# Gated cross attention and mixture of experts: weights and token kept behind each quarter of a row, slot loads on one queue, the last gates by TensorE

## The chip, the cores and the metric

The kernel runs on one core of a Trainium2 chip. The metric is the device time of one execution in microseconds, the median of three runs. A core has a matrix engine (TensorE, PE), a vector engine (VectorE, DVE), a scalar engine (ScalarE, ACT), a general engine (GpSimd, POOL) and a sync engine (SyncE, SP). Each has its own instruction stream and works through it in order; they wait for each other with semaphores. Transfers are issued by SP, ACT and POOL and carried by 16 DMA engines.

## The reference

`x` is 4 x 2048 x 512 in float32, 8192 tokens in all; the context is 4 x 77 x 512. A gated cross attention with 16 heads of 64 is followed by a gated mixture of 8 true and 2 null experts, of which each token takes the best two.

```python
x = x + tanh(g_xattn[0]) * xattn(layernorm(x), ctx)      # q, k, v, softmax over 77 keys, w_out, b_out
h = layernorm(x)
logits = h @ gate_w.T + gate_b                           # 10 columns: 8 experts, 2 null
weights, selected = top_k(softmax(logits), 2)
true = weights * (selected < 8)
combine = one_hot(selected) * true / max(sum(true), ...)  # per token and expert
x = x + tanh(g_ffn[0]) * sum_e combine[:, e] * (h @ expert_w[e] + expert_b[e])
```

## The kernel before, in words

**First phase.** Keys are folded into the query weights and values into the output weights, so that one tile of 128 tokens needs only two groups of matmuls: scores (line 281, four chunks of 512 by 1232 columns) and the attention output (line 360, ten chunks into one PSUM bank, `attend`). There are 64 tiles; `step(i)` works on several at a time: scores of tile i+1, attend of tile i-1, gates of tile i-2. The order of all instructions is written out by hand (`manual_schedule`), so each engine's order is the order of the calls. The softmaxed scores are transposed in 32 x 32 squares by VectorE and put in place by 16 small transfers from SP (`attn_move`, line 353).

**Gates and buckets.** After the residual (line 373) and its store, tile i's normalised row is written by ScalarE into one of nine row buffers of 528 columns (`norm_apply`, line 255): 512 of data, then two weights and the token number. `gate_logits` (line 382) makes ten products with reductions on VectorE, one per gate; `choose` finds the best two, `ratio` and `weigh` make the weights, `place` (line 453) counts with two small matmuls, `dispatch` computes row numbers and scatters the rows of two tiles into two buckets in HBM, `hb[0]` for first choices and `hb[1]` for second (line 475, GpSimd, indirect). Each bucket has room per expert, so rows of one expert stand together.

**Second phase.** Rows are worked in slots of 128 rows of one expert: 118 of them, 59 of the first choices and then 59 of the second. Each pass ends with eight "part" slots whose rows are gathered through an index. `early_table`, `first_table` and `second_table` compute on VectorE where each slot starts and which expert it has. For a slot: `slot_load` brings its rows from `hb`, in an arrangement that makes VectorE's 32 x 32 transpose (`slot_tr`, line 943) a full one; `slot_acc` gathers the tokens' present output (line 925, GpSimd); `slot_pe` makes four matmuls of 512 columns (line 981); `slot_out` adds bias, scales and adds (lines 989, 990, VectorE); `slot_put` scatters the result (line 997, GpSimd). Part slots are transposed by TensorE with two ScalarE copies (lines 952 to 958).

A full slot's load is five transfers: one for the columns behind the data (line 902) and four for the quarters of 128 columns (line 905). After slot 8 two of the quarters go by ScalarE's queue. There are eleven slot buffers: seven row buffers and four pieces of the softmax buffers; loads are issued five slots ahead, transposes two.

**Hand-over.** The first slots need only tiles up to SNAP (57), so slots 0 to 3 are mixed with attend 62 and 63. In this stretch VectorE makes the gate products of tiles 61 and 62, and `tail(q)` does tile 63's, two products per slot, its dispatch and the first table at q = 8, the second table at q = 12 and the part table at q = 14.

Of the kernel before, what the change touches and what calls it, by code (L numbers as in the profile page):

```python
# [8 lines left out]
F32 = mybir.dt.float32  # L9
# [15 lines left out]
def kernel(  # L25
# [112 lines left out]
    for n in range(2):  # L138
        a = const.tile([P, NKC * P], F32, name=f"attn{n}")
        nc.gpsimd.memset(a[:, COLS:], 1.0)  # L140
        attns.append(a)
    rows = []
    for n in range(NRB):
        r = const.tile([P, ROW], F32, name=f"row{n}")
        nc.gpsimd.memset(r[:, D:], 0.0)
        rows.append(r)

    nc.gpsimd.memset(rows[0][:, :D], 0.0)
    nc.gpsimd.memset(rows[0][:, D + 2 : D + 3].bitcast(I32), BIG)
# [103 lines left out]
    def norm_apply(key, dst, src):  # L253
        rs, nb = norms.pop(key)
        nc.scalar.activation(dst, src, AF.Identity, bias=nb, scale=rs)

# [120 lines left out]
    def gate_logits(i, e0, e1):  # L377
        if e0 == 0:
            pgs[i] = stile("pg", i, NG)
        for e in range(e0, e1):  # L380
            prod = work.tile([P, D], F32, tag="prod", name=f"prod_{i}_{e}", bufs=1)
            nc.vector.tensor_tensor_reduce(  # L382
                prod,
                hrs[i][:, :D],
                gwb[:, e, :],
# [5 lines left out]
            )  # L391

# [5 lines left out]
    def choose(i):  # L398
# [25 lines left out]
        nc.gpsimd.tensor_copy(hrs[i][:, D + 2 : D + 3].bitcast(I32), tokid[:, i : i + 1])  # L424
# [9 lines left out]
    def weigh(m):  # L434
# [9 lines left out]
        for b in range(2):  # L444
            nc.vector.tensor_scalar(
                hrs[2 * m + b][:, D : D + 2], w2[:, b], rd[:, b : b + 1], gf, ALU.mult, ALU.mult
            )

    def place(m):

        pps[m] = pp = mm_tile(f"pp{m}")
# [9 lines left out]
    def dispatch(m):  # L461
# [10 lines left out]
        for i in (2 * m, 2 * m + 1):  # L472
            hr = hrs.pop(i)
            for k in range(2):
                ins = nc.gpsimd.indirect_dma_start(  # L475
                    out=hb[k],
                    out_offset=bass.IndirectOffsetOnAxis(ap=dst[:, i % 2, k : k + 1], axis=0),
                    in_=hr[:, :].bitcast(I32),
                    in_offset=None,
                    bounds_check=NROWS - 1,  # L480
                    oob_is_err=False,
                )
                tc.declare_no_dep(ins.ins, group="scatter", reason="rows of one bucket differ")
                tc.add_to_no_dep_group("scatter", ins.ins)
                if i > SNAP:
                    tc.declare_no_dep(ins.ins, group="block", reason="blocks full by tile SNAP")
                    tc.add_to_no_dep_group(f"late{i}", ins.ins)
# [185 lines left out]
    def step(i):  # L673
# [14 lines left out]
        if i == NT - 2:  # L688
            slot_tr(0)
            slot_tr(1)  # L690
# [26 lines left out]
        if is_tile(i - 1):  # L717
            norm_shift(f"h{i - 1}")
            hrs[i - 1] = rows[(i - 1) % NRB]
            norm_apply(f"h{i - 1}", hrs[i - 1][:, :D], x1s.pop(i - 1))  # L720
# [53 lines left out]
    scr = m_flat[:, 6 * D :]  # L774
    assert NT * (2 * NE + 1) <= NC * COLS - 6 * D

    def count_rows(cs):
        pc = mm_tile("pc")
# [92 lines left out]
    ring += rows[NRB - 3 : NRB - 1]  # L871
    px_pool = []
    hss, metas, toks, accs, hsTs, exps, pes, turn = {}, {}, {}, {}, {}, {}, {}, [0, 0]

    def slot_load(n):
# [3 lines left out]
        metas[n] = hs[:, D:]  # L879
# [9 lines left out]
        else:  # L889
            both = n > N1 // 2  # L890
            queues = (nc.sync, nc.scalar) if both else (nc.sync,)
            r = nc.values_load(
                starts[t][0:1, s : s + 1],
                engines=[ENG.SP, ENG.Activation] if both else [ENG.SP],
# [7 lines left out]
            loads = [queues[0].dma_start(hs[:, D:].bitcast(I32), block[:, D:])]  # L902
            for g in range(4):
                loads.append(
                    queues[g // 2 * (len(queues) - 1)].dma_start(  # L905
                        hs[g * 32 : (g + 1) * 32, :D]
                        .rearrange("p (j d) -> p j d", j=4)
                        .bitcast(I32),
                        block[:, g * P : (g + 1) * P].rearrange("(j a) d -> a j d", a=32),
                    )  # L910
                )
            if t == 0:
# [6 lines left out]

    def slot_acc(n):  # L920
        k = order[n][0]
        tok = metas[n][:, 2:3].bitcast(I32)
# [272 lines left out]
```

## Time and profile before

| | us |
|---|---|
| runs | 1693.61, 1693.76, 1691.02 (median 1693.61) |
| profiled execution | 1677.89 |
| its span | 1676.2 |
| granted TensorE clock, mean | 0.993 |
| one slot on TensorE (distance between starts) | 3.43 |
| one attend on TensorE | 8.59 |

The profile is of one execution. A line of instructions in time has start, duration, engine, line, operation, output<-input, shape and count, and in brackets the idle time before it with what ended it. A line of a group has the busy total, the mean duration in ns and the idle time before it. TensorE's busy time holds overlapping durations (a group of eight records shows 3.60 where the next starts 3.43 later), so distances between starts are used.

### The profile page before, as it was taken

To read this page: it belongs to the slowest core of one execution; us is meant where nothing else is said; L and a number is where in the kernel's file an instruction comes from. 1 tells how busy PE (TensorE), PEld (TensorE's weight loads), DVE (VectorE), ACT (ScalarE), POOL (GpSimd) and SP (SyncE) were. 2 spreads that over 40 slices of the span, in tenths; PEclk is the share of its full clock that TensorE was granted. 3 is DMA by queue.
4 is the path that set the end of the run, shared out by engine and by line. 5 is a ranking of instruction groups with operands and counts; after the bars stand their busy time and mean duration, and the time that the engine had idled before them with its cause. 6 is when DMAs were issued, how large, how long until landed. Compare 5 with 4: busy or idle time off the path is not lost.

```text
span 1676.2 us, 23173 instructions
## 1 busy us (share of the span) xinstructions
PE 1635.7 (98%) x4530; PEld 809.5 (48%) x4530; DVE 1293.8 (77%) x3324; ACT 884.2 (53%) x3188; POOL 466.9 (28%) x617
## 2 busy tenths in 40 slices
PE   8899999999999999999999999999988999999997
PEld 6544455454544545455454554545433444444443
DVE  1554999899898998989899898998988755466653
ACT  2464777777777777767777677776620000100001
POOL 4031111112111211112111121111226656575565
PEclk9999999999999999999999999999998999999999
DMA  7468443346533445644333566655447986688862
GB/s 236 177 198 228 105 98 87 85 104 162 153 89 85 107 94 144 154 93 107 88 94 88 154 169 145 162 139 160 112 112 229 266 242 187 173 255 235 233 189 78
DMA packets 484934, 252.07 MB, mean 150 GB/s; under 512 B 369509, under 2 KB 425829, under 8 KB 484529
## 3 DMA queue, kind: packets, MB, share of 16 engines
q1 hardware_dynamic: 423473, 134.77, 34.4%
q0 software_dynamic: 34528, 103.55, 18.8%
q10 hardware_dynamic: 26784, 12.20, 3.0%
q14 instruction: 109, 0.89, 0.2%
q8 instruction: 40, 0.66, 0.2%
HBM read 119.41 MB, written 100.52 MB: 131 GB/s over the span
## 4 chain that ended last, share of the span: by engine, by line
PE 85%; DVE 5%; DMA 3%; SPq 3%; issue 2%; ACT 1%; POOL 1%; POOLq 0%; DVEq 0%; ACTq 0%
PE po L360 29%; PE sc L281 29%; PE px L981 11%; PE pe L981 10%; PE pv L622 2%; SPq L353 2%; DVE prod L382 2%; PE pkv L519 2%; PE xtr L261 2%; DMA vw_all<-row 1%; DMA gwb<-in_L_ffn_gate_w_dram 1%; DMA x<-in_x_dram 0%; DMA row<-hb 0%; SPq L905 0%; PE pm L597 0%
## 5 line engine op out<-in xcount | busy, mean ns | idle before, releaser
L360 PE MATMUL po<-vw,aT 128*128 128x512 f32 (+1 forms) x1280 | 561.8, 594 | 2.6 <-issue 2.4
L281 PE MATMUL sc<-m_sb,xnT 128*128 128x385 f32 (+1 forms) x1536 | 552.9, 510 | 0.0
L382 DVE CUSTOM_DVE_ANT_0 prod<-row,gwb,gbias 128x512 f32<-128x512 f32 x640 | 478.3, 747 | 25.2 <-DMA gwb<-in_L_ffn_gate_w_dram 7.3
L360 PEld LDWEIGHTS po<-vw,aT 128*128 128x128 f32 (+1 forms) x1280 | 243.8, 191 | 305.3 <-issue 301.9
L281 PEld LDWEIGHTS sc<-m_sb,xnT 128*128 128x128 f32 x1536 | 283.9, 190 | 212.5 <-issue 86.1
L475 POOL DMA_INDIRECT hb<-row,dst x128 | 128.1, 1001 | 752.1 <-DVE nbh_h L250 673.0
L314 ACT ACTIVATE attn<-sc,nmx 128x77 f32<-128x77 f32 x1024 | 316.0, 346 | 35.0 <-DVE nmx L309 31.3
L314 ACT ACTIVATION_READ_ACCUMULATOR attn<-sc,nmx 128x1 f32 x1024 | 232.8, 227 | 0.0
L981 PE MATMUL px<-big,m_sb 128*128 (+1 forms) x472 | 215.1, 599 | 10.7 <-DVE m_sb L943 10.4
L981 PE MATMUL pe<-big,m_sb 128*128 (+1 forms) x472 | 212.5, 593 | 1.0 <-DVE m_sb L943 1.0
L981 PEld LDWEIGHTS px<-big,m_sb 128*128 128x128 f32 x472 | 89.7, 192 | 121.7 <-issue 109.2
L981 PEld LDWEIGHTS pe<-big,m_sb 128*128 128x128 f32 x472 | 88.8, 190 | 110.1 <-issue 106.4
L303 DVE TENSOR_REDUCE mx<-sc 128x5 f32<-128x385 f32 (+1 forms) x192 | 106.2, 580 | 20.2 <-PE sc L281 18.1
L233 ACT ACTIVATE sdh_h<-mvh_h,eps_t 128x1 f32<-128x1 f32 x64 | 18.9, 295 | 187.7 <-DVE rsa_a L245 178.5
L989 DVE TENSOR_TENSOR yb<-pe,blks 128x512 f32<-128x512 f32 x59 | 40.6, 688 | 76.9 <-PE pe L981 76.9
L952 ACT COPY m_sb<-row 128x512 f32<-128x512 f32 x11 | 6.8, 620 | 176.4 <-DVE acc L990 174.5
L264 ACT ACTIVATE xnT<-xtr,bet,gam 128x128 f32<-128x128 f32 x256 | 95.4, 452 | 7.4 <-PE xtr L261 7.4
L989 DVE TENSOR_TENSOR yb<-px,blks 128x512 f32<-128x512 f32 x59 | 40.6, 688 | 76.0 <-PE px L981 74.6
L327 DVE TENSOR_TENSOR attn<-attn,ri 128x1232 f32<-128x1232 f32 x64 | 92.3, 1443 | 5.1 <-DMA aT<-attn 0.8
L997 POOL DMA_INDIRECT out_dram<-acc,row x75 | 76.2, 1016 | 65.1 <-DVE acc L990 52.2
L336 DVE STREAM_TRANSPOSE attn<-attn 128x1248 f32<-128x1248 f32 x64 | 94.2, 1471 | 0.0
L373 DVE SCALAR_TENSOR_TENSOR x<-po,gx,x 128x512 f32<-128x512 f32 x64 | 48.0, 750 | 58.0 <-PE pp L453 34.5
(163 smaller groups left out, 1540.1 us busy)
## 6 DMA issues: line engine op xcount, KB each, us to landing
aT<-attn SPq DMA_DIRECT2D x768, 40.0 KB
x<-in_x_dram SPq DMA_DIRECT2D x64, 256.0 KB
out_dram<-x SPq DMA_DIRECT2D x64, 256.0 KB
aT<-attn SPq DMA_DIRECT2D x256, 36.0 KB
row<-hb SPq DMA_DIRECT2D x138, 64.0 KB
big<-in_L_ffn_expert_w_dram SPq DMA_DIRECT2D x32, 256.0 KB
row<-hb ACTq DMA_DIRECT2D x118, 64.0 KB
vw<-vw_all SPq DMA_DIRECT2D x9, 768.0 KB
```

What stands on the lines that cost most here:

```text
L264: nc.scalar.activation(xnT[:, c, :], ptr[:, c, :], AF.Identity, bias=bet[:, c : c + 1], scale=gam[:, c : c + 1],)
L281: nc.tensor.matmul(t[:, : n1 - n0], xnTs[i][:, c, :], m_sb[:, c, n0:n1], start=(c == 0), stop=(c == NC - 1),)
L303: nc.vector.tensor_reduce(mx[:, g0:g1], scs[i, g][:, : (g1 - g0) * SK].rearrange("p (h k) -> p h k", k=SK), AX.X, ALU.max,)
L314: nc.scalar.activation(a[:, h * SK : (h + 1) * SK], t[:, k : k + SK], AF.Exp, bias=nm[:, h : h + 1], scale=SCALE, accum_out=sm[:, h : h + 1],)
L327: nc.vector.tensor_tensor(a, a, ri.unsqueeze(2).to_broadcast([P, H, SK]), ALU.mult)
L336: nc.vector.transpose(a[:, :n], a[:, :n])
L360: nc.tensor.matmul(po, aT[:m, k, :], vw[:m, k, :], start=(k == 0), stop=(k == NKC - 1),)
L382: nc.vector.tensor_tensor_reduce(prod, hrs[i][:, :D], gwb[:, e, :], 1.0, gbias[:, e : e + 1], ALU.mult, ALU.add, pgs[i][:, e : e + 1],)
L475: ins = nc.gpsimd.indirect_dma_start(out=hb[k], out_offset=bass.IndirectOffsetOnAxis(ap=dst[:, i % 2, k : k + 1], axis=0), in_=hr[:, :].bi ...
L981: nc.tensor.matmul(pe, hsT[:, c, :], w[:, c, :], start=(c == 0), stop=(c == NC - 1))
L989: nc.vector.tensor_tensor(tt, pe, b, ALU.add)
L997: ins = nc.gpsimd.indirect_dma_start(out=of, out_offset=bass.IndirectOffsetOnAxis(ap=tok, axis=0), in_=acc, in_offset=None, bounds_check=T ...
```

## The change

- A row is now four quarters of 132 columns: 128 of data, two weights, the token, one unused. The weights and the token are written behind each quarter (`weigh`, `choose`), the token as a float. Everything that reads or writes the data of a row uses a view of four pieces.
- A full slot's load is four transfers of 132-column quarters, all by SP. A new `slot_meta` copies, on ScalarE, the pieces behind the quarters to the place of the first one and turns the token to an integer.
- There are twenty slot buffers (nine pieces of the value buffer are added); loads are issued nine slots ahead, transposes of full slots four.
- The gates of tiles 61, 62 and 63 are made by TensorE: the gate weights are transposed once before step 4, and for each tile `gate_transpose` and `gate_product` are called in the hand-over.
- The order of the hand-over is new: slot 1 after attend 62, loads of slots 3 to 6 after the moves of tile 63, tile 63's dispatch before slot 6 with its four scatters spread over q = 1 to 4, the tables at q = 3, 6 and 9. Small counts use the transpose banks, and slots use the two kinds of PSUM bank in groups of three.

```diff
+    QC = D // 4
+    QR = ROW // 4
+    def quarters(r):
+        return r.rearrange("p (i d) -> p i d", d=QR)
...
+    def norm_row(i):
+        hrs[i] = rows[i % NRB]
+        norm_apply(
+            f"h{i}",
+            quarters(hrs[i])[:, :, :QC],
+            x1s.pop(i).rearrange("p (i d) -> p i d", i=4),
+        )
...
             nc.vector.tensor_tensor_reduce(
-                prod,
-                hrs[i][:, :D],
-                gwb[:, e, :],
+                prod.rearrange("p (i d) -> p i d", i=4),
+                quarters(hrs[i])[:, :, :QC],
+                gwb[:, e, :].rearrange("p (i d) -> p i d", i=4),
...
+    def setup_gate():
+        rows10 = rows[NRB - 1][:, :D]
+        ptr = tr_tile("gwtr")
+        for c in range(NC):
+            nc.tensor.transpose(ptr[:, c, :NG], rows10[:NG, c * P : (c + 1) * P], ident[:NG, :NG])
+        nc.vector.tensor_copy(gwT, ptr[:, :, :NG])
+
+    def gate_transpose(i):
+        ptr = tr_tile(f"gtr{i}")
+        for c in range(NC):
+            nc.tensor.transpose(ptr[:, c, :], quarters(hrs[i])[:, c, :QC], ident)
+        nc.scalar.copy(hgT, ptr)
+
+    def gate_product(i):
+        pl = tr_tile(f"gl{i}")[:, 0, :NG]
+        for c in range(NC):
+            nc.tensor.matmul(pl, hgT[:, c, :], gwT[:, c, :], start=(c == 0), stop=(c == NC - 1))
+        pgs[i] = stile("pg", i, NG)
+        nc.vector.tensor_tensor(pgs[i], pl, gbias, ALU.add)
...
+    ring += [vw_flat[:, v * ROW : (v + 1) * ROW] for v in range(NKC * D // ROW)]
...
-            both = n > N1 // 2
-            queues = (nc.sync, nc.scalar) if both else (nc.sync,)
...
-            loads = [queues[0].dma_start(hs[:, D:].bitcast(I32), block[:, D:])]
-            for g in range(4):
-                loads.append(
-                    queues[g // 2 * (len(queues) - 1)].dma_start(
...
+            loads = [
+                nc.sync.dma_start(
+                    quarters(hs)[g * 32 : (g + 1) * 32].bitcast(I32),
+                    block[:, g * QR : (g + 1) * QR].rearrange("(j a) d -> a j d", a=32),
                 )
+                for g in range(4)
+            ]
...
+    def slot_meta(n):
+        if n in toks:
+            return
+        hs = hss[n]
+        metas[n] = hs[:, QC:QR]
+        if order[n][1] is not None:
+            for g in range(1, 4):
+                r = slice(g * 32, (g + 1) * 32)
+                nc.scalar.copy(hs[r, QC:QR], quarters(hs)[r, g, QC:])
+        toks[n] = hs[:, QR + QC : QR + QC + 1].bitcast(I32)
+        nc.scalar.copy(toks[n], metas[n][:, 2:3])
...
-        if q < 5:
-            gate_logits(i, 2 * q, 2 * q + 2)
-        elif q == 5:
-            choose(i)
-            ratio(i)
-        elif q == 8:
-            weigh(i // 2)
-            place(i // 2)
-            pc = count_rows(csum[0][:, 0])
-            dispatch(i // 2)
-            first_table(pc)
-        elif q == 12:
+        if 0 < q <= len(later):
+            put_rows(*later[q - 1])
+        if q == 3:
+            first_table(count_rows(csum[0][:, 0], flat_tr("pclast")))
+        elif q == 6:
             second_table()
-        elif q == 14:
+        elif q == 9:
             part_table()
...
         slot_pe(0)
-        slot_pe(1)
+        slot_tr(1)
         slot_tr(2)
-        slot_tr(3)
         for i in (NT - 2, NT - 1):
-            gate_logits(i - 1, 0, NG)
             attend(i)
-            choose(i - 1)
-            ratio(i - 1)
+            gate_transpose(i - 1)
             residual(i)
             norm_stats(f"h{i}", x1s[i])
             norm_root(f"h{i}")
+            slot_pe(1 if i == NT - 2 else 3)
+            gate_product(i - 1)
+            norm_shift(f"h{i}")
+            norm_row(i)
+            choose(i - 1)
+            ratio(i - 1)
             if i == NT - 2:
                 weigh(i // 2 - 1)
-                place(i // 2 - 1)
+                place(i // 2 - 1, flat_tr("pp"))
                 dispatch(i // 2 - 1)
...
+                slot_pe(2)
+                for n in range(3, 7):
+                    slot_load(n)
+                slot_tr(3)
         for n in range(4):
             slot_acc(n)
-        tail(0)
+        for n in range(7, 10):
+            slot_load(n)
+        gate_transpose(i)
+        slot_tr(4)
+        slot_tr(5)
+        slot_pe(4)
         slot_out(0)
+        slot_put(0)
+        slot_out(1)
+        gate_product(i)
+        choose(i)
+        ratio(i)
+        slot_pe(5)
+        weigh(i // 2)
+        place(i // 2, flat_tr("pplast"))
+        dispatch(i // 2, later)
         for q in range(1, M + 1):
-            if 1 < q < M - 5:
-                slot_load(q + 5)
-            slot_put(q - 1)
+            if q + 9 < M:
+                slot_load(q + 9)
+            if q > 1:
+                slot_put(q - 1)
...
-            if 1 < q < M - 2:
-                slot_tr(q + 2)
-            if 2 < q < M:
+            for n, whole_tile in ((q + 4, True), (q + 2, False)):
+                if 5 < n < M and whole_tile == (order[n][1] is not None):
+                    slot_tr(n)
+            if 5 < q < M:
                 slot_pe(q)
-            if q < M:
+            if 1 < q < M:
                 slot_out(q)
```

## The prediction

> **What bounds the kernel now.** I read the busy table first, then TensorE's instructions in order of time around the hand-over from the attention tiles to the expert slots, then the table by stage, then what VectorE did in TensorE's gaps.
>
> ```profile
> PE 1635.7 (98%) x4530; PEld 809.5 (48%) x4530; DVE 1293.8 (77%) x3324; ACT 884.2 (53%) x3188; POOL 466.9 (28%) x617
> 200.00:600.00 400.00, 400.00 (x1129) 201.99 (x1128) 361.98 (x1015) 300.45 (x1108) 61.59 (x99) 1.00 0.45 108
> 1260.00:1280.00 20.00, 17.68 (x35) 7.70 (x36) 18.18 (x40) 1.58 (x2) 14.41 (x14) 0.81 0.75 226
> 1500.00:1550.00 50.00, 50.00 (x117) 22.06 (x117) 29.52 (x43) 0.00 (x0) 30.02 (x30) 1.00 0.82 238
> ```
>
> In the three lower lines the columns are length, then busy time of TensorE, weight loads, VectorE, ScalarE and GpSimd, then granted clock, DMA share and GB/s. TensorE has no gap in the attention steps or the settled slots. It loses time in one place only, the hand-over:
>
> ```profile
> 1219.64 3.60 PE L981 MATMUL px<-big,m_sb 128*128 x8
> ...
> 1236.05 0.18 PE L453 MATMUL pp<-msk,upper 128*128 128x40 bf16 x1 [0.79 <-DVE msk L412]
> ...
> 1249.14 3.60 PE L981 MATMUL pe<-big,m_sb 128*128 x8
> 1262.32 6.28 PE L981 MATMUL px<-big,m_sb 128*128 x8 [9.59 <-DVE m_sb L943]
> 1268.44 3.60 PE L981 MATMUL pe<-big,m_sb 128*128 x8
> ...
> 1290.33 3.67 PE L981 MATMUL pe<-big,m_sb 128*128 x8 [0.97 <-DVE m_sb L943]
> ```
>
> Slot 0 starts at 1219.64 and slot 11 at 1290.33, so 70.69 us. Eleven slots at 3.43 (the steady distance between starts) are 37.77 and two attends at 8.59 are 17.18; the excess is **15.7 us**. It is the 9.59 gap, 2.85 for the slot after it (6.28 instead of 3.43, granted clock 0.81), 0.97 before slot 11, about 1.3 around 1236, and small pieces. VectorE explains the gap: from 1227 to 1272 it mostly makes gate products for the last three tiles:
>
> ```profile
> L382 DVE CUSTOM_DVE_ANT_0 prod<-row,gwb,gbias 128x512 f32<-128x512 f32 x640 | 478.3, 747 | 25.2 <-DMA gwb<-in_L_ffn_gate_w_dram 7.3
> 1261.56 0.71 DVE L943 STREAM_TRANSPOSE m_sb<-row 128x512 f32<-128x512 f32 x1
> ```
>
> Ten products at 0.80 are 8 us a tile, and slot 4's transpose stands behind them and behind two slot results that wait for gathers.
>
> **Part 1, gates of tiles 61 to 63 by TensorE.** VectorE loses 3 x 8 = 24 us. TensorE gains, per tile, four transposes and four matmuls. Four transposes cost 0.44 us (row below). A matmul with 10 moving columns is not in the trace; in fp32 each shows as two records with two weight loads, so eight per tile.
>
> ```profile
> 1170.63 0.60 PE L261 MATMUL xtr<-ident,y 128*128 128x128 f32 x4
> 1171.07 5.85 PE L281 MATMUL sc<-m_sb,xnT 128*128 128x385 f32 x16
> 1236.56 0.30 PEld L981 LDWEIGHTS px<-big,m_sb 128*128 128x128 f32 x2 [0.41 <-issue]
> L281 PEld LDWEIGHTS sc<-m_sb,xnT 128*128 128x128 f32 x1536 | 283.9, 190 | 212.5 <-issue 86.1
> ```
>
> With so few columns the weight load sets the pace. [...] The trace's fp32 loads take 190 ns alone (1.5 us a tile) and 0.30 for two back to back. I take 0.15 each, since these will be back to back: 1.2 us, ends 0.85 and 1.5. Three tiles: 3 x (0.44 + 1.2) = **4.9 us**, ends 3.9 and 5.8. [...] The four transposes of the gate weights before step 4 are on a full TensorE: **+0.44** (below 0.44 if ten partitions are quicker; nothing hides them).
>
> **Part 2, the new order.** I followed it by hand. TensorE: slot 0, attend 62, transposes 61, slot 1, product 61, counts, slot 2, attend 63, transposes 62, slot 3, product 62, transposes 63, slot 4, product 63, slot 5, counts, slot 6 onward. It is full except where VectorE's answer to a small product is waited for; each hand-off is summed from rows (gap to a reader 0.25, bias add 0.18, the two shift operations 0.37, top-8 and mask 0.7, ScalarE's row 0.82, transpose 0.71):
> - A: product 61, add, shift of tile 62, choose, counts: 0.25+0.18+0.37+0.7 = 1.5.
> - B: product 62, add, shift, tile 63's row on ScalarE, its transposes: 0.25+0.18+0.37+0.05+0.82+0.1 = 1.75. Queued behind it are slots 4 and 5.
> - C: counts of the last pair, dispatch (0.4), slot 6's transpose, slot 6: about 1.5.
> - D: the first table now stands before slot 8's transpose. It took 1285.09 to 1289.47, 4.4 us; VectorE has slot 8 ready about 1.7 after TensorE could use it.
> - E: the second table (1298.87 to 1303.42, 4.6) before slot 11's: 1.0.
>
> Sum 7.45. No gap reaches a third of the 9.59 that brought the clock down (the 0.97 gap did not: 3.67 follows), so I charge nothing for clock. New excess: 4.9 + 7.45 + 0.3 for counts = 12.6, against 15.7: **gain 3.1**. The ends: hand-offs fully covered gives 10.5; each half as long again takes it to -0.6.
>
> Other engines here: the loads of slots 3 and 4 move behind the 16 moves of tile 63 on SP, and slots 0 to 2 issue 12 transfers instead of 15, so the moves for 62 and 63 start some 1.6 and 3 us sooner and attend 63 (not before 1241) no longer waits for them (0.22 at 1240). Slot 3 is loaded from about 1236 and read near 1241. Gathers still wait for the last residual store. The four last scatters, 1.3 us each on GpSimd, are spread between puts; GpSimd then has 4 x 1.3 to make up at 3.43 - 2.6 = 0.8 a slot, and gathers run three slots (10 us) ahead. Slot 16, the first to need them landed, is due on TensorE near 1304.
>
> **Part 3, the middle.** When the second pass starts, gathers wait for the last put:
>
> ```profile
> 1468.68 0.75 DVE L990 SCALAR_TENSOR_TENSOR acc<-yb,row,acc 128x512 f32<-128x512 f32 x1 [5.49 <-DMA acc<-out_dram,row]
> 1470.11 3.70 PE L981 MATMUL px<-big,m_sb 128*128 x8 [0.78 <-DVE m_sb L943]
> ```
>
> Transposes will be four slots ahead instead of two, and the six banks hold slots 59 to 63 (17 us), more than the 5.49: **gain 0.9**. Another 0.15 before the start at 1304.19 goes with the tables.
>
> **Part 4, rows and loads.** Per slot five transfers become four, all on SP. In one slot (1204.36 to 1207.31) SP took 2.95 for five; less 0.55 it is 2.4, under 3.43, so no cost; cover gone, each 0.1 us over would be 12 us in 118 slots. ScalarE issues none but makes four small copies a slot, at 0.30 (the 128x1 row of line 233) 1.2 of 3.43 us; it is otherwise empty there. The loads run nine slots ahead, so even a copy delayed by a part slot's is covered. For the DMA engines, q10 carries only such loads: 3.0% x 16 x 1676 / 26784 = 30 ns a packet; 512 of these a slot are 15.4 of 16 x 3.43 = 54.9 engine-us, and the 128 weight packets (q1's mean, 22 ns) another 2.8. By the row the share falls from 0.82 to 0.77.
>
> ```profile
> q1 hardware_dynamic: 423473, 134.77, 34.4%
> q10 hardware_dynamic: 26784, 12.20, 3.0%
> ```
>
> [...] Rows are 2112 B apart. [...] The 528 B transfer itself is unseen: from 15.4 engine-us to double.
>
> The attention steps get products, ScalarE rows and GpSimd copies on four pieces of 128. The trace's nearest rows show no price for pieces (ScalarE's copy in 32-column pieces, line 952, 620 ns; plain, line 958, 590). VectorE has 400 - 362 = 38 us free in 23 steps, 1.65 a step, 0.165 a product: cost 0 up to there.
>
> **Sum**: -3.1 - 0.9 - 0.15 + 0.44 = **-3.7 us** of the profiled 1677.9 (span 1676.2). The median of runs shown, 1693.61, lies 15.7 above that; I carry this unchanged: 1689.9, say **1690**. 0.2% (3.4 us) is about what a measurement of this kernel can tell from no change.
>
> **Rivals.**
> - Hand-offs mostly covered (TensorE finds its work ready at C, D, E): -7 to -11, 1685. For: VectorE is lighter by 24 us. Against: both tables still stand in the chain, earlier.
> - Transposes wait for ScalarE's copies into the same row: slots 4 and 6 lose about 1.2 us each at the hand-over, and B grows past 3 us, so the clock falls as at 1262 (2.85): -3.7 + 2.4 + 2.85 = +1.5, 1695. Against: line 353's 16 moves into interleaved columns of one buffer run 0.65 apart, without waiting for each other.
> - Slower: **the loads cannot keep pace**. One queue with odd quarters: if a 528 B packet costs double, a slot needs 45 (0.82 x 54.9) + 15.4 - 2.8 = 58 of 54.9 engine-us, 3.6 us, and 118 x 0.17 less the 3.7 gives +16, 1710. It decides from about 54 ns a packet, or from 3.43 us of SP per slot.
> - A product on pieces over 0.165 us slower makes VectorE the bound: each 0.1 beyond is 10 x 0.1 x 60 = 60 us, 1740 or more.
>
> **How the numbers follow.** The sum's case 0.48 (own range 1687 to 1692.5, three quarters of it past the 0.2%); covered hand-offs 0.20; copies in the way 0.12 (a third of it slower); loads 0.14; products 0.06. Faster 0.37 + 0.20 = 0.57, same 0.11 + 0.08 = 0.19, slower 0.24. Range 1684 to 1702: below it a part of the second case, above it most of loads and products.
>
> **What would show it.** Right: no TensorE gap over 2 us after 1219, granted clock 1.00 throughout, L990's wait at the middle with no gap on TensorE, slot starts 3.43 apart, DMA share about 0.8 in the slots. Wrong: slot starts over 3.43 apart (loads), VectorE over 95% in the steps (products), eight small matmuls over 1.5 us, or a gap near slot 4 or 8 over 3 us.

## The result and the profile after

The changed kernel took **1702.3 us** (median of eight, 1696.8 to 1704.6), the kernel before 1693.8 (eight, 1688.6 to 1698.1) in the same comparison: ratio 1.0049, 95% interval 1.0031 to 1.0066. That is 8.3 us slower; 1690 was forecast, and 1702.3 lies just above the range. The execution profiled here took 1696.8, the fastest of the eight.

The busy line of the page, and the table by stage (length, busy time of TensorE, weight loads, VectorE, ScalarE and GpSimd, granted clock, DMA share, GB/s):

```profile
PE 1646.2 (97%) x4570; PEld 814.3 (48%) x4570; DVE 1270.2 (75%) x3268; ACT 964.0 (57%) x3615; POOL 472.0 (28%) x617
```

```profile
200.00:600.00 400.00, 400.00 (x1129) 201.97 (x1128) 361.63 (x1017) 299.38 (x1106) 63.78 (x99) 1.00 0.45 109
1260.00:1280.00 20.00, 17.57 (x49) 8.10 (x48) 15.73 (x43) 7.00 (x37) 11.41 (x13) 0.98 0.72 211
1500.00:1550.00 50.00, 50.00 (x117) 22.05 (x117) 29.75 (x46) 7.63 (x40) 33.90 (x32) 1.00 0.75 224
1400.00:1450.00 50.00, 39.75 (x96) 17.00 (x95) 20.43 (x30) 10.06 (x39) 32.85 (x31) 0.93 0.74 212
1600.00:1650.00 50.00, 45.21 (x112) 20.09 (x110) 24.92 (x37) 8.00 (x37) 34.77 (x34) 1.00 0.69 209
```

The last two stages in the kernel before:

```profile
1400.00:1450.00 50.00, 50.00 (x142) 23.78 (x141) 23.93 (x34) 9.23 (x16) 36.71 (x35) 1.00 0.58 173
1600.00:1650.00 50.00, 50.00 (x135) 23.26 (x135) 25.18 (x36) 7.25 (x13) 35.64 (x35) 1.00 0.52 164
```

The attention steps are unchanged and 1500 to 1550 is full. The granted clock in 1260 to 1280 is 0.98 for 0.81; the clock is still halved in the hand-over (0.50 granted), but for 3.4 us (from 1257.5) instead of 10.2 (from 1257.3). TensorE loses time in two new places, 10 us in 1400 to 1450 and 5 us in 1600 to 1650, where it was full before. The hand-over in order of time:

```profile
1220.57 3.60 PE L1043 MATMUL px<-big,m_sb 128*128 x8
...
1236.47 0.95 PE L427 MATMUL gl<-gwT,m_sb 128*128 128x10 f32 x8
1238.52 0.19 PE L498 MATMUL pp<-msk,upper 128*128 128x40 bf16 x1 [1.10 <-DVE msk L450]
...
1257.36 1.02 PE L421 MATMUL gtr<-ident,row 128*128 128x128 f32 x4 [1.37 <-issue]
1258.17 4.96 PE L1043 MATMUL pe<-big,m_sb 128*128 x8
1262.97 0.96 PE L427 MATMUL gl<-gwT,m_sb 128*128 128x10 f32 x8
1263.78 3.68 PE L1043 MATMUL pe<-big,m_sb 128*128 x8
...
1268.72 7.13 PE L1043 MATMUL px<-big,m_sb 128*128 x16 [1.20 <-DVE m_sb L1005]
1277.09 3.70 PE L1043 MATMUL px<-big,m_sb 128*128 x8 [1.24 <-DVE m_sb L867]
```

The 9.59 gap is gone; four gaps of 1.10 to 1.37 stand in its place. Then TensorE at the end of the first pass:

```profile
1405.86 7.03 PE L1043 MATMUL pe<-big,m_sb 128*128 x16
1416.70 5.40 PE L1043 MATMUL pe<-big,m_sb 128*128 x8 [3.81 <-DVE m_sb L1005]
...
1436.21 0.66 PE L1019 MATMUL str<-ident,gwb 128*128 128x128 f32 x4 [1.15 <-ACT vw L979]
...
1444.09 0.66 PE L1019 MATMUL str<-ident,gwb 128*128 128x128 f32 x4 [3.79 <-issue]
1444.59 5.29 PE L1043 MATMUL pe<-big,gwb 128*128 128x512 f32 x8
```

Slot 47 starts 3.81 late and runs at a lowered clock (0.50 granted from 1417.9 to 1421.3; the next starts 5.24 later instead of 3.43), and the slots after it lose more. To see where time goes over all 118 slots I took the first of the eight matmul records of each slot in each trace, and the difference to the start of the same slot in the trace of before. Executions enter this stage a few us apart, so read each row's differences along the row; the last column is slot 117's start less slot 0's.

```
start of slot:       0     11     16     46     48     51     56     63    108    117   0 to 117
before           1219.6 1290.3 1307.7 1410.7 1417.6 1429.2 1448.6 1473.7 1628.6 1662.6    442.9
after, minus it    0.93  -2.64  -2.69  -1.43   4.35   7.50  13.48  12.43  12.43  19.25    461.2
```

From slot 0 to 11 the change gains 3.57 us, from 56 to 63 (the middle) 1.05. It loses 1.3 between 16 and 46, 14.9 between 46 and 56, and 6.8 at slots 109 and 110. From 63 to 108 all slots are 3.43 apart. What is late at slot 47 stands in VectorE's row, and what is late for VectorE in SyncE's (start, time to the last of the group, count):

```profile
1415.93 0.71 DVE L1005 STREAM_TRANSPOSE m_sb<-attn 128x512 f32<-128x512 f32 x1 [5.87 <-DMA attn<-hb]
```

```profile
1386.40 8.81 SPq L954 DMA_DIRECT2D row<-hb  x13
1396.72 19.10 SPq L954 DMA_DIRECT2D attn<-hb  x16
```

Sixteen transfers, four slots, took SyncE 19.10 us, 4.8 a slot, while TensorE uses up a slot in 3.43. One number did not fit from the start: the trace of before is of an execution of 1677.9 us, and none of that kernel's eight other executions in this comparison is under 1688.6. The experiments had to say where those 11 to 20 us are.

### The profile page after: what moved, and what is told of

The parts are those of the page before. It is cut to its first block, busy times and chain, and to the rows that moved or that the text cites. A ratio compares the mean times of both kernels' runs of the same rounds, so it can differ in the third digit from the quotient of the medians.

```text
span 1695.1 us, 23666 instructions
## 1 busy us (share of the span) xinstructions
PE 1646.2 (97%) x4570; PEld 814.3 (48%) x4570; DVE 1270.2 (75%) x3268; ACT 964.0 (57%) x3615; POOL 472.0 (28%) x617
## 3 DMA queue, kind: packets, MB, share of 16 engines
q1 hardware_dynamic: 435589, 146.99, 36.8%
## 4 chain that ended last, share of the span: by engine, by line
PE 75%; issue 7%; DMA 5%; SPq 4%; DVE 3%; another core or an unknown queue 2%; ACT 2%; POOL 2%; POOLq 0%; DVEq 0%; ACTq 0%
PE po L375 31%; PE sc L296 30%; PE px L1043 4%; PE pe L1043 3%; SPq L954 3%; PE pv L673 2%; PE pkv L570 2%; PE xtr L276 2%; POOL acc L986 1%; DMA row<-hb 1%; DVE prod L397 1%; DMA vw_all<-row 1%; POOL out_dram L1059 1%; DMA out_dram<-acc,row 1%
## 5 line engine op out<-in xcount | busy, mean ns | idle before, releaser
L397 DVE CUSTOM_DVE_ANT_0 prod<-row,gwb,gbias 128x512 f32<-128x512 f32 x610 | 455.6, 747 | 22.6 <-DMA gwb<-in_L_ffn_gate_w_dram 7.3
L1043 PE MATMUL px<-big,m_sb 128*128 x424 | 188.1, 598 | 2.7 <-DVE m_sb L867 1.2
L1043 PE MATMUL pe<-big,m_sb 128*128 x392 | 175.6, 602 | 4.4 <-DVE m_sb L1005 3.8
L1043 PEld LDWEIGHTS px<-big,m_sb 128*128 128x128 f32 x424 | 80.5, 191 | 102.8 <-issue 98.4
L1043 PEld LDWEIGHTS pe<-big,m_sb 128*128 128x128 f32 x392 | 74.9, 193 | 100.4 <-issue 92.3
L318 DVE TENSOR_REDUCE mx<-sc 128x5 f32<-128x385 f32 (+1 forms) x192 | 106.3, 581 | 18.6 <-PE sc L296 16.6
L262 ACT ACTIVATE row<-x,nbh_h,rsh_h 128x512 f32<-128x512 f32 x64 | 52.1, 814 | 64.5 <-DVE nbh_h L257 62.0
L977 ACT COPY vw<-vw 32x4 f32<-32x4 f32 x111 | 21.2, 191 | 117.3 <-DMA vw<-hb 95.3
```

The source lines that it names most:

```text
L318: nc.vector.tensor_reduce(mx[:, g0:g1], scs[i, g][:, : (g1 - g0) * SK].rearrange("p (h k) -> p h k", k=SK), AX.X, ALU.max,)
L397: nc.vector.tensor_tensor_reduce(prod.rearrange("p (i d) -> p i d", i=4), quarters(hrs[i])[:, :, :QC], gwb[:, e, :].rearrange("p (i d) -> ...
L1043: nc.tensor.matmul(pe, hsT[:, c, :], w[:, c, :], start=(c == 0), stop=(c == NC - 1))
```

## The experiments

Theories: **one queue** (the transfers are too much for SyncE's queue), **depth** (nine slots ahead crowds it), **GpSimd** (three indirect transfers a slot at the end of a pass), **rows** (the 528 B pieces and ScalarE's copies), later **crowd** (the number of all engines' instructions), **SyncE alone** (its own number of instructions) and **chip**. The runs were made in five sets; the kernels of a set ran on one chip beside the kernel before, which took 1697.5, 1678.9, 1694.7, 1680.4 and 1698.5 us in them. Each set had a chip of its own: numbers 9, 11, 14, 7 and 3. Which chip the first comparison and the first profile of the kernel before ran on is not known. The changed kernel itself ran only in sets 3 and 4. In the other sets a variant is compared with it through the kernel before, that is, from one chip to another.

| set | kernel | median us | ratio to before, 95% |
|---|---|---|---|
| 1 | two_queues | 1696.4 | 0.9996 (0.9984 to 1.0008) |
| 1 | parts_five | 1707.7 | 1.0063 (1.0043 to 1.0083) |
| 1 | lead_five | 1706.1 | 1.0056 (1.0040 to 1.0073) |
| 1 | old_rows | 1702.1 | 1.0028 (1.0014 to 1.0042) |
| 2 | fixed_both | 1673.6 | 0.9965 (0.9953 to 0.9977) |
| 2 | fixed_expert | 1674.8 | 0.9971 (0.9959 to 0.9983) |
| 2 | before_one_queue | 1677.6 | 0.9992 (0.9982 to 1.0001) |
| 2 | before_again | 1679.5 | 1.0003 (0.9993 to 1.0013) |
| 3 | after_again | 1701.8 | 1.0045 (1.0026 to 1.0063) |
| 3 | fixed_both_2 | 1687.0 | 0.9960 (0.9944 to 0.9976) |
| 3 | two_queues_2 | 1698.7 | 1.0016 (0.9994 to 1.0038) |
| 3 | before_again_2 | 1693.7 | 0.9998 (0.9979 to 1.0016) |
| 4 | **after_again_3** | 1675.3 | **0.9974 (0.9965 to 0.9984)** |
| 4 | fixed_rows | 1676.2 | 0.9975 (0.9965 to 0.9986) |
| 4 | fixed_expert_2 | 1674.5 | 0.9964 (0.9951 to 0.9978) |
| 4 | fixed_extra | 1674.1 | 0.9965 (0.9952 to 0.9979) |
| 5 | fixed_rows_2 | 1693.4 | 0.9963 (0.9950 to 0.9977) |
| 5 | fixed_extra_2 | 1692.5 | 0.9963 (0.9949 to 0.9976) |

### Set 1: queue, depth, GpSimd, rows

**two_queues** gives half of the loads back to ScalarE.

```diff
-                nc.sync.dma_start(
+                queues[g // 2 * (len(queues) - 1)].dma_start(   # SyncE, ScalarE from slot 9 on
```

> The changed kernel, but from slot 9 on two of the four quarter loads are issued by ScalarE again. Theory one queue: in the changed kernel SyncE falls into stretches where each of its instructions takes 0.7 us (about 240 such steps between 1250 and 1620 us, 18 before the change), loads come late, and slots 47 to 53 lose 14.9 us; with half of the loads on ScalarE those stretches shrink to under 60 steps and the time falls by 8 to 15 us against the changed kernel, to 1687 to 1694. Theory GpSimd: the losses come from GpSimd, which has three indirect transfers of 1.33 us per slot (4.0 us) while slots come every 3.43 us; then the time stays within 3 us of the changed kernel, 1699 to 1705.

Equal to before, so beside the 1.0049 of the first comparison it leans to one queue's side, though 1696.4 is above its 1694. Slot 47 is not late in this trace (the row at slot 48 stands where it stood at 16), but the ends of the passes still lose, and slots 14 to 16 do too:

```
start of slot:       0     11     16     46     48     51     56     63    108    117   0 to 117
two_queues         1.92  -2.71   2.10   2.10   2.10   6.50  12.63  11.59  11.59  16.87    457.9
old_rows           0.48  -2.73   2.05   2.05   3.95   4.41  13.48  12.44  12.44  22.59    465.0
parts_five         2.65   1.03   2.60   5.86   5.86  18.34  20.79  19.75  24.85  29.26    469.5
lead_five          0.84  -0.63   0.74   5.82   6.11  23.17  24.39  23.34  23.52  27.41    469.5
```

**parts_five** and **lead_five** shorten the lead, of the part slots' loads and of all.

```diff
-            if q + 9 < M:
-                slot_load(q + 9)
+            for n, whole_tile in ((q + 9, True), (q + 5, False)):     # parts_five
+                if 9 < n < M and whole_tile == (order[n][1] is not None):
+                    slot_load(n)
...
+            if 9 < q + 5 < M:                                         # lead_five
+                slot_load(q + 5)
```

> The changed kernel, but the eight loads of part slots in each pass (GpSimd) are issued five slots ahead instead of nine, as before the change; all other loads stay nine ahead on SyncE. Theory GpSimd: five of the eight then fall on slots of 3.87 us, the backlog at the end of a pass shrinks from 4.6 to about 2.4 us, the losses at slots 49 to 53 and 109 to 110 (10 and 6.8 us in the profile) mostly go, and the time falls to 1688 to 1694. Theory one queue: slot 47 still waits for its load and the second loss stays small in the median, time 1698 to 1704.

> The changed kernel, but from slot 10 on every load is issued five slots ahead instead of nine. Theory depth (many loads outstanding crowd the queue): the 0.7 us stretches of SyncE go to under 60 steps and the time falls to 1688 to 1694. Theory one queue: SyncE still issues all four loads, has a shorter lead to live on, and the time is the same or worse, 1701 to 1712. Theory GpSimd: as with part loads alone five ahead, 1688 to 1694.

Neither gain came: 1.0063 and 1.0056 are not below 1.0049 (the intervals overlap, so they are not shown to be slower than the changed kernel either). Depth and GpSimd fall in the form that I gave them. TensorE, then ScalarE and GpSimd of parts_five at the first part slot:

```profile
1435.07 1.11 PE L1019 MATMUL str<-ident,gwb 128*128 128x128 f32 x4 [8.03 <-issue]
```

```profile
1434.31 0.19 ACT L979 CAST vw<-vw 128x1 int32<-128x1 f32 x1 [3.10 <-DMA vw<-hb,pidx]
1434.41 0.61 ACT L1014 COPY gwb<-vw 128x512 f32<-128x512 f32 x1
```

```profile
1426.11 1.17 POOL L934 DMA_INDIRECT vw<-hb,pidx  x1 [0.31 <-issue]
...
1430.25 1.02 POOL L934 DMA_INDIRECT vw<-hb,pidx  x1 [0.30 <-issue]
```

TensorE stands 8.03 us until the part slot's copy at 1434.41, behind a small cast that waits for the second part load, issued at 1430.25. GpSimd's transfers went out one after another there, 1.3 to 1.5 us apart from 1426.11 to 1430.25, and at 1406.85 a put, with all that stands behind it, had waited 1.83 us for VectorE's result; so a lead counted in GpSimd's slots is worth less to TensorE when VectorE is behind. That speaks for the lead of nine, but does not prove it.

**old_rows** keeps the hand-over, buffers and leads, and takes back the rows and the five loads on two queues.

```diff
-        return r.rearrange("p (i d) -> p i d", d=QR)
+        return r[:, :D].rearrange("p (i d) -> p i d", d=QC)
...
+            loads = [queues[0].dma_start(hs[:, D:].bitcast(I32), block[:, D:])]
```

> The changed kernel with the row layout and loads of the kernel before (weights and token once behind the row, five loads per slot, from slot 9 on shared by SyncE and ScalarE, no copies by ScalarE), but the gates by TensorE, the new order, the twenty buffers and the lead of nine. My sum for the hand-over and the middle: 3.1 + 0.9 + 0.15 - 0.44 = 3.7 us under the kernel before, so ratio 0.998 and about 1690. Theory GpSimd: part loads nine ahead still cost, so the gain is eaten and the time is 1694 to 1702. Theory one queue or rows: no loss at the ends of the passes, 1688 to 1692.

1.0028: the gain at slot 11 is there (-2.73), and it is lost at the same places. So the rows are not needed for the loss, and neither is one queue. How much each adds is not shown, since the interval of this ratio and that of the changed kernel overlap (1.0014 to 1.0042, 1.0031 to 1.0066).

### Set 2: the same places, with nothing lost

**fixed_both** and **fixed_expert** write what a slot reads from the tables into the code.

```diff
-            r = nc.values_load(starts[t][0:1, s : s + 1], engines=[ENG.SP], ...)
-            block = hb[k][bass.ds(r, P), :]
+            r = (FIXED[t] + [NROWS] * NT)[s]                # fixed_both, fixed_rows
+            block = hb[k][r : r + P, :]
...
-            e = nc.values_load(which[t][0:1, s : s + 1], engines=[ENG.PE, ENG.DVE], ...)
+            e = (EXPERT[t] + [NE - 1] * NT)[s]              # fixed_both, fixed_expert
```

> The changed kernel with each full slot's row block and expert written into the code instead of read from the tables (the tables are still made; the transfers, matmuls and their order are the same, the register instructions go: on SyncE some 9 of 16 instructions a slot, on TensorE 5, on VectorE 2). Theory crowd (the engines are held up together, whenever the instruction streams are dense: SyncE and ScalarE step in turn every 0.73 us while others stand): fewer instructions, fewer such stretches, the time falls by 8 to 17 us against the changed kernel, to 1685 to 1694. Theory one queue (the transfers themselves are too many for one queue): packets and queue are the same, time within 3 us of the changed kernel, 1699 to 1706.

> The changed kernel with only the expert of each full slot written into the code; the row blocks are still read from the tables, so SyncE has all of its instructions and transfers, and TensorE and VectorE lose 5 and 2 register instructions a slot. Theory crowd: a part of the gain of the run without both, 3 to 8 us under the changed kernel, 1694 to 1699. Theory SyncE alone (only its own number of instructions counts): no change, 1700 to 1705.

**before_one_queue** sets `both = False` in the kernel before; **before_again** changes nothing.

> The kernel before with all five loads of every slot on SyncE and none on ScalarE. Theory one queue: SyncE's 2.95 us a slot grow into 0.7 us steps as in the changed kernel, the lead of five slots is used up, and the time is 8 to 20 us above the kernel before, ratio 1.005 to 1.012. Theory crowd: the number of instructions is the same as before, only their place differs: within 3 us, ratio 0.998 to 1.002.

> The kernel before once more, unchanged, for a second trace of it: its profiled execution took 1677.9 us where its other executions took 1688 to 1698. If those others also have stretches in which SyncE takes 0.7 us a step and slots that start late, the 16 us between them lie in the slots after 1250 us, and the attention steps are the same to 1 us. If not, slots are 3.43 us apart here too, and the 16 us lie elsewhere, spread over the execution.

The kernel before takes 1678.9 in this set, 18.6 less than in set 1, and none of the four traces has a late slot after the hand-over: from slot 16 to 117 each row of starts moves only at the middle. All loads on SyncE cost the kernel before nothing here (0.9992); one queue had asked for 1.005 to 1.012. These runs can't tell crowd from chip, since the changed kernel is not among them.

### Set 3: the changed kernel beside its variants

> The changed kernel once more, unchanged. The kernel before took 1693.8 and 1697.5 us in two comparisons and 1678.9 in a third, on another chip, where no slot was late in any of the four kernels tried. Theory chip: the late slots belong to the chip. Where the kernel before takes about 1679, the changed kernel has its slots 3.43 us apart and comes out at my sum, ratio 0.997 to 0.999; where the kernel before takes 1693 to 1698, the ratio is 1.003 to 1.007 and slots 47 to 53 and 109 to 110 are late again. Theory kernel: the loss belongs to the change, the ratio is 1.003 to 1.007 on every chip.

> The changed kernel with row blocks and experts of the full slots written into the code, a second time, beside the changed kernel on the same chip. Theory crowd (dense instruction streams bring on the late slots): where the changed kernel has late slots, this one has few, and is 8 to 17 us below it. Theory one queue: within 3 us of it. Where the changed kernel has none, it is within 2 us of it.

> The changed kernel with two of the four loads of a slot on ScalarE, a second time, beside the changed kernel on the same chip. Theory one queue: 4 to 10 us below the changed kernel where that has late slots, the same to 1.5 us where it has none. Theory crowd: its instructions are 2 a slot more than the changed kernel's, so not below it by more than 2 us on any chip.

> The kernel before a third time, for its trace on this chip. Theory chip: where its time is above 1690, its own slots are late too at places after 1250 us, 10 to 18 us together; where it is about 1679, none is.

```
start of slot:       0     11     16     46     48     51     56     63    108    117   0 to 117
before_again_2     1.58   1.86   6.33   6.33   6.33   6.33  12.69  12.66  12.66  16.62    458.0
after_again        1.04  -0.57  -0.70   2.31   4.31  14.95  21.96  20.92  20.92  29.63    471.5
fixed_both_2       0.50  -3.41  -3.53  -3.53  -3.53  -3.53   1.12   0.08   0.08   8.40    450.8
```

That is where the 16 us of the kernel before are: on this chip **it has late slots too**, at slots 15 and 16, 52 and 53, 111 and 112, 14.8 us from slot 11 to 117. The changed kernel has 30.2 in this trace, of its slowest execution (1707.5), and 21.9 in the first one, of its fastest. With blocks and experts in the code it is 14.8 us faster in the median (1701.8 to 1687.0). two_queues_2 lies 3.1 below the changed kernel, a little short of what one queue asked for, and the two ratios' intervals overlap.

SyncE's load instructions show what differs; columns: count, then shortest/median/longest ns. The changed kernel first:

```profile
L954 SPq FUSED_REGOPS  x408: 3/46/1395, 1201.7 to 1617.5; - x136
L954 SPq EVENT_SEMAPHORE  x186: 2/28/717, 1201.8 to 1615.3; - x186
L954 SPq MOVE attn<-hb x96: 3/29/1397, 1242.7 to 1614.5; - x96
...
  DVE m_sb L1005: 46.3, 21
```

The last line says that VectorE's transposes waited 46.3 us for these loads, 21 times. In after_again, a second trace of the changed kernel, that line, one of these waits and SyncE's transfers around it are:

```profile
  DVE m_sb L1005: 47.2, 22
1430.55 0.71 DVE L1005 STREAM_TRANSPOSE m_sb<-row 128x512 f32<-128x512 f32 x1 [6.98 <-DMA row<-hb]
1401.15 18.67 SPq L954 DMA_DIRECT2D attn<-hb  x16
1424.10 6.22 SPq L954 DMA_DIRECT2D row<-hb  x8
```

The transfer waited for was issued after 1424.10, behind sixteen others that took 18.67, and slot 49 starts 9.4 late there. So in both traces of the changed kernel that have slow stretches, late loads from SyncE come first at the end of the first pass. The view of before_again_2, then of before_again:

```profile
L905 SPq MOVE row<-hb x138: 3/29/708, 1203.3 to 1616.7; - x138
```

```profile
L905 SPq MOVE row<-hb x138: 29/29/38, 1202.5 to 1604.3; - x138
```

In the first trace of before a MOVE on SyncE takes 29 ns, 42 at most; in some stretches of other traces it, and SyncE's transfers and register operations with it, go in steps of 0.7 us (in the changed kernel's starts at 1510.07, 1510.78, 1511.50, 1512.21 and 1512.91). MOVEs over 0.5 us on SyncE after 1200 us: 44 of 408 in the changed kernel, 39 in after_again, 18 of 324 in before_again_2, and none in the first trace of before or in those of sets 2 and 4. The changed kernel's longest wait for a semaphore there is 0.717 us, so SyncE was never ahead of its buffers.

TensorE's 408 register operations after 1200 us take at most 60 ns in every trace that has them, so not all engines go in such steps. The transfers themselves are no slower: between 1250 and 1620 us a 528 B packet takes 34.3 ns on average in the changed kernel and 35.3 in its undisturbed trace of set 4 below. Nor is the fetching of the instructions (the page's queues of kind instruction, q8 and q14): 168 such packets in either trace, and after 1200 us a median of 429 ns against 512.

Late loads do not explain the late slots of the kernel before: its transposes wait 1.0 us in all for them in before_again_2. Nor do they explain what is left in two_queues_2 and fixed_both_2, where no transpose waits for them.

### Set 4: the changed kernel where the kernel before takes 1680

> The changed kernel once more, unchanged, as the base of this comparison. Theory chip: if the kernel before takes about 1679 us here, the changed kernel is at 1674 to 1677 (ratio 0.997 to 0.999) with slots 3.43 us apart; if it takes 1693 to 1698, ratio 1.003 to 1.007 with late slots. Theory kernel: 1.003 to 1.007 either way.

> The changed kernel with only the row blocks of the full slots written into the code: 9 of SyncE's 16 instructions a slot go, TensorE and VectorE keep theirs. Where the changed kernel has late slots: theory SyncE alone says it gets all of the gain of the run with both, 10 to 15 us below the changed kernel; theory crowd says about the share of its instructions (9 of 16), 5 to 10 us; theory one queue says nothing, within 3 us. Where it has none: the same to 2 us under all three.

> The changed kernel with only the expert of each full slot written into the code: TensorE loses 5 and VectorE 2 instructions a slot, SyncE none. Where the changed kernel has late slots: theory SyncE alone says the same to 3 us; theory crowd 4 to 8 us below the changed kernel. Where it has none: the same to 2 us.

**fixed_extra** is fixed_both with work added to ScalarE:

```diff
+            for j in range(8):
+                nc.scalar.copy(idle[:, j : j + 1], eps_t)
```

> Row blocks and experts written into the code, and eight small ScalarE copies (128x1, into a tile that nobody reads) added to every slot: 1.6 us of ScalarE's 3.43, with nothing waiting for them. Where the changed kernel has late slots: theory crowd says that half of the gain of the run without them is lost again, 4 to 10 us above its 14.8 us below the changed kernel; theory SyncE alone says the whole gain stays, 12 to 17 us below the changed kernel. Where it has none: the same to 2 us.

The changed kernel is **faster** here, 0.9974, 5.1 us by the medians, and the four kernels lie within 2.1 us of each other. Two stages and SyncE's row of after_again_3:

```profile
1400.00:1450.00 50.00, 50.00 (x142) 23.65 (x141) 22.93 (x33) 11.34 (x33) 36.38 (x36) 1.00 0.81 228
1600.00:1650.00 50.00, 50.00 (x135) 23.24 (x134) 23.93 (x34) 8.07 (x21) 38.21 (x36) 1.00 0.52 164
```

```profile
L954 SPq FUSED_REGOPS  x408: 42/46/56, 1203.1 to 1573.1; - x136
L954 SPq EVENT_SEMAPHORE  x186: 17/28/10927, 1203.2 to 1571.5; - x186
```

The same code, and no register operation over 56 ns. SyncE waits up to 10.9 us for a buffer to come free: it is ahead, the last load goes out at 1573, and TensorE is full in both stretches. Theory chip stands: the same code is slower than the kernel before on chip 14 and faster on chip 7. Each chip was used in one set only, so chip and time of the run are not separated; and on chip 14 one of twelve executions of two_queues_2 took 1684.0 where the others took 1693.4 to 1703.2.

### Set 5: which instructions count

> The changed kernel with only the row blocks of the full slots written into the code, a second time. If the kernel before takes 1690 or more here: theory SyncE alone says all of the gain of the run with both, ratio 0.994 to 0.998; theory crowd says about 9 of 16 parts of the way from 1.0047 to 0.996, 0.999 to 1.002; theory one queue says 1.003 to 1.007. If it takes about 1680: 0.997 to 0.998 under all.

> Row blocks and experts written into the code, and eight small ScalarE copies added to every slot, a second time. If the kernel before takes 1690 or more here: theory crowd says 4 to 10 us lost of the run without them, ratio 0.998 to 1.002; theory SyncE alone says that nothing is lost, 0.994 to 0.997. If it takes about 1680: 0.996 to 0.997 under both.

The kernel before takes 1698.5 here. With only SyncE's register work gone the whole gain is there (0.9963, like 0.9960 with both on chip 14), and with eight more instructions a slot on ScalarE it is there too (0.9963). Crowd had asked for 0.998 or more in both, so it misses twice and **SyncE alone** hits twice. These ratios are held against those of other chips, though: neither the changed kernel nor fixed_both ran on this one, and by the bare number of instructions the two variants are nearly equal (9 fewer a slot than the changed kernel, and 16 fewer with 8 added). What does not hang on that is the wait: no transpose waits for SyncE's loads in the traces of fixed_rows_2, fixed_extra_2 and fixed_both_2. SyncE in fixed_rows_2 still has slow stretches:

```profile
L950 SPq EVENT_SEMAPHORE  x186: 3/28/10704, 1203.1 to 1585.1; - x186
L950 SPq DMA_DIRECT2D vw<-hb x148: 3/430/1191, 1266.4 to 1552.5; - x148
```

but with 6 instead of 15 instructions in a slot's load (two waits counted) it gets ahead again (a wait of 10.7 us, last load 1585 instead of 1617). Fixed blocks take away the register instructions and the transfers' register addresses together; which of the two matters was not separated. The single traces of this set are no proof of where the rest goes: fixed_rows_2 still loses 11 us between slots 51 and 56 and fixed_extra_2 16 between 48 and 51, and the latter was that kernel's slowest execution (1697.2). All traces of sets 1, 3 and 5 lose at the ends of the passes. There GpSimd has no pause, as in the changed kernel:

```profile
1622.12 1.02 POOL L934 DMA_INDIRECT vw<-hb,pidx  x1 [0.30 <-issue]
1623.45 1.01 POOL L1059 DMA_INDIRECT out_dram<-acc,row  x1 [0.30 <-issue]
1624.76 1.29 POOL L986 DMA_INDIRECT acc<-out_dram,attn  x1 [0.30 <-issue]
1626.35 1.02 POOL L934 DMA_INDIRECT vw<-hb,pidx  x1 [0.31 <-issue]
```

A part load, a put and a gather take 4.2 us from 1622.12 to 1626.35, and a slot takes 3.43. In the traces of sets 2 and 4 no slot is late at these places. Why it costs there, and why a stretch comes when it does, stays open.

## Why the prediction was wrong

**Gates by TensorE (Part 1)**: right in kind, a little dear. Eight records of a gate product take 0.81 us (1262.97 to 1263.78; 1266.31 to 1267.12 in after_again_3) where I took 1.2. No run shows the 0.85 that I put at the lower end; in its place the runs showed this 0.81. The weight load set the pace, as taken: a record of 10 columns took 0.10 (a slot's of 512 take 0.43), and seven of the eight loads stand end to end (0.86 from 1262.97), where those of a slot have 0.24 between them. Three tiles cost 3 x (0.44 + 0.81) = 3.8, not 4.9. The transposes of the gate weights, forecast at 0.44, make the distance between two attends 0.40 longer there.

**Hand-offs (Part 2)**: the sum held, its terms partly cancelled. A, B, C and D measured 1.10, 1.37, 1.20 and 1.24 for 1.5, 1.75, 1.5 and 1.7, and E none for 1.0: 4.9 instead of 7.45. Against that, "I charge nothing for clock" failed: after the 1.37 gap the next start came 4.80 us after the slot's in the changed kernel's trace and 5.23 in after_again_3, 1.4 and 1.8 us more than 3.43, and there the slot after the 1.10 gap took 5.23 too. (By the same measure slot 4 of the kernel before cost 2.69, not the 2.85 of the prediction, which took a duration less a distance.) From slot 0 to 11 took 67.1 us in the changed kernel and 69.1 in after_again and after_again_3, for 70.7 before: gains of 3.6, 1.6 and 1.6 for the 3.1 forecast. That the total came near is partly luck: gates and hand-offs were cheaper, the clock dearer. The rival of covered hand-offs did not come.

**The middle (Part 3)**: 1.05 for 0.9, in all three traces of the changed kernel, against the first trace of before; that kernel's own start of the second pass moves by 0.5 in before_again.

**Rows and loads (Part 4)**: this is one step that failed. The pieces are harmless, as taken: products stay at 747 ns, ScalarE's small copies take 0.19, and a 528 B packet takes 34.3 to 35.3 ns on average (512 B before: 31.9 and 32.3 on the two queues), nowhere near the 54 of the rival. The 64 B pieces that went away took 10.7 ns, not the 22 of a mean over all packets of a queue, so a slot's packets take 17.6 engine-us after 17.8, and the DMA share, for which I took 0.77 by the row, stayed at 0.82 (1500 to 1550 of after_again_3, as before). SyncE's 2.4 us a slot is near, too, where it runs undisturbed: 0.51 us a load, and 2.7 a slot in the median of after_again_3 with its table read. But "under 3.43, so no cost" rested on SyncE's pace in a trace without slow stretches. Where it has them a slot took 4.8 us (1396 to 1416), the lead of nine was used up, and slot 47 was late. The rival **loads cannot keep pace** named the point, "3.43 us of SP per slot"; its price was worked out from packets, whose work stayed the same, and not from SyncE's instructions.

**The carry-over** is the other: "The median of runs shown, 1693.61, lies 15.7 above that; I carry this unchanged". The runs that took those 15.7 us left no trace; before_again_2, of the same length, has 14.8 us of late slots from slot 11 on, and the changed kernel has 21.9 and 30.2 in its two traces with slow stretches. An undisturbed trace gave the sum, and the sum is about right for an undisturbed chip: 1680.4 - 3.7 = 1676.7 for 1675.3 measured, though the slots of after_again_3 show only 2.8 of the gain (442.9 to 440.1). Where there are slow stretches it is right for the hand-over and the middle and misses some 12 us, 8.3 + 3.7. As much goes away when the register work of the slots is left out: fixed_both_2 is 14.8 us below the changed kernel on the same chip, and fixed_rows_2, without SyncE's alone, stands as well against the kernel before on another. The warning stood in the table of times: a profiled execution 0.8 to 0.9% below the three others, four times my sum, in places that its profile couldn't show.

## What to carry to other kernels

When the profiled execution is further from the others than the change is worth (here 15.7 us against 3.7), the profile may lack a cost, and a second trace is worth more than a finer sum. SyncE's time per slot was not a constant here (2.7 us in the median of after_again_3, 4.8 in the changed kernel's trace from 1396 to 1416): count an issuing engine's instructions, register work for dynamic addresses included, and keep the load path well under the pace of the slots, here 3.43 us. Before a version is called slower or faster by half a per cent, measure it on more than one chip, with the kernel before beside it.

## What was unexpected of the hardware

- The same two kernels compare as 1.0045 (1.0026 to 1.0063) on chip 14 and as 0.9974 (0.9965 to 0.9984) on chip 7. Of the five numbered chips three take 1694.7 to 1698.5 for the kernel before and two take 1678.9 and 1680.4. What differs between them was not found.
- In one slow stretch VectorE and ScalarE stood too. In the changed kernel's trace TensorE's slot 69 ends at 1510.1 and its result is taken up by VectorE only at 1514.44, after 5.41 idle; ScalarE goes on at 1514.43, after 4.97, and SyncE's 0.7 us steps end at 1514.35. How SyncE's stretch and their waits hang together was not found.
- Traces of sets 1, 3 and 5 hold fewer records of semaphore updates: 13.6 per us between 1300 and 1350 in before_again_2 against 41.5 in before_again, 10.3 in the changed kernel's first trace against 36.8 in after_again_3. They hold fewer already in the attention steps, where nothing is slower (18.6 against 21.4 per us between 200 and 600). Fewer records and late slots stand in the same traces; whether the recording has a part in the slow stretches was not shown, since no run here turns the records off.
- After a gap of 1.10 or 1.37 us the clock was halved for 3.4 us in some executions (0.50 granted from 1257.5 to 1260.9 in the changed kernel's trace, 0.91 on average in 1260 to 1280 of after_again_3), and the slot there took 4.8 or 5.2 us; in the trace of before a gap of 0.97 had no such effect (1.00 granted, next start 3.51 later). The gaps stand in stretches of 2.6 and 3.1 us that hold only small products and transposes (1236.47 to 1239.04 and 1255.03 to 1258.17 in the hand-over shown above); whether the gap or the whole stretch counts was not tested, and after the first of these two the clock stayed full in that trace (1.00 from 1239.0 to 1242.5).
